# Attention on one core: queries and new keys turned by VectorE and a trip through DRAM in place of TensorE, with the second values' product, the token sums and the keys' norms moved

## The chip, the cores and the metric

The kernel is one launch on one core of a Trainium2 chip. The metric is device time in microseconds, the median of several runs. Beside it there is one profiled execution, with the times of every instruction; times of single instructions below are from it.

## What is computed

Four layers work on x, 8 blocks of 128 tokens with 512 features, and the result of each is added to x: low-rank adapters and a gated MLP, a second pair of adapters, attention with a paged cache followed by a routed low-rank layer, and a last pair. The change lies in the attention of the third layer:

```python
q = x @ Wq.T   # 32 heads of 128;  k, v: 8 heads
q, k = rope(rmsnorm(q) * qw), rope(rmsnorm(k) * kw)
kc, vc = k_cache[block_table], v_cache[block_table]      # 512 cached rows for each block
k_all, v_all = concat(kc, k), concat(vc, v)              # 640 keys, each used by 4 heads
scores = q . k_all / sqrt(128), cached rows from the block's length on set to -1e30
o = softmax(scores) . v_all
y = o @ Wo.T
```

rmsnorm divides each head's vector by the root of its mean square. All data are float32.

## The kernel before

The attention is a loop over 32 steps n in `run` (L1176). A step is one head group qd of 8 (one key head, four query heads) and one pair p of 4 (two blocks of 128 tokens, j = 0 and 1). Step n works on three steps' data at once:

- `weigh(n, j)` (L1066): scores of block j, transposed. For each of five chunks c of 128 keys, a product of the keys (features by keys, as weights) with the queries of four heads (features by 512) into a PSUM tile `st`, then Exp on ScalarE into `pT` (L1074). Chunks 0 to 3 are cached keys `kT`, chunk 4 the new keys `kn`.
- `added` (L1080): four VectorE adds over the five chunks into `part`. `divisors` (L1088): a product with ones (`sum`, L1094), reciprocal, four copies R (L1102), and three copies of R between partitions by DMA on SP's queue, then one of the sums.
- `mix(n, j)` (L1108): five products of values with `pT` into `av`, then one VectorE multiply by R into `oT` (L1116). `outputs`: VectorE sums `os` of oT.
- `project(n+1)` (L953): queries, keys and values of the next step, by a Strassen-like scheme of seven block products (`seven`, L915; tiles q_one, q_six, q_five), VectorE adds the parts (L936, L937, L968). Its token-side sums `xs` come from `tokens` (L910), four VectorE adds, in every step.
- `leave(n-1)` (L1125): the same scheme with Wo (tiles wo_one, wo_two, wo_six), added into y by VectorE (L1135) and GpSimd (L1138, L1143). Between its products `rotate(n+1)` (L986) is placed: GpSimd's and VectorE's halves of the rotation (L997, L1001) and ScalarE's squares.
- `normed(n+1)` (L1019): ScalarE's Sqrt, VectorE adds rk+vk and rq+vq (L1025), reciprocal, and a multiply of keys and of queries by it (L1029).
- `turn_cached(n+1)` (L1032): the gathered cached keys are transposed by VectorE in 32x32 blocks (L1038, tile `kt`), written to DRAM by four DMAs on SP's queue (L1042) and read back as whole transposes by one (L1045, `kT`).
- `turn(n+1)` (L1048): new keys and queries are transposed by TensorE against the identity (kTn, L1053: 2; qTp, L1060: 8), copied out of PSUM by VectorE (L1055) and ScalarE (L1062).
- `gather` (L883): eight indirect DMAs of GpSimd for values, eight for cached keys.

Tiles come from pools with a number of buffers for each tag; a new tile waits for the last user of the buffer that it takes. The order of instructions on each engine is set when the program is built: a scheduler reorders them by its own estimates, and `kept` (L847) pins an instruction to the program's order among the pinned ones of its engine.

## Time and profile before

| | us |
|---|---|
| median of 3 runs (1638.76 to 1641.55) | 1640.6 |
| the profiled execution's own time | 1622.67 |
| its span, first to last instruction | 1620.4 |
| TensorE's 8 + 2 transposes in a step: 256 of 0.280 each, 64 of 0.299; busy in all | 40.2 + 13.9 |
| ScalarE's copies qT, 64 of 0.586 | 37.5 |
| VectorE's copies kTs, 32 of 0.362 | 11.6 |
| VectorE's multiply of keys (L1029), 32 of 0.681 | 21.8 |
| VectorE's token sums xs (L907), three rows | 26.6 + 13.6 + 13.4 |
| VectorE's transposes of cached keys (L1038), 64 of 0.687 | 41.6 |
| TensorE waits for part before sum (L1094) | 19.2 in 23 waits |

The attention loop takes from about 336 us to about 1460 us of the span. A row of groups gives an instruction's line, engine, output and inputs, shape, count, busy time in all and the mean of one. An instruction's own length overlaps with its successor's on the same engine: the pitch from one start to the next is shorter (a float32 product with 512 columns is two instructions of 0.592 us at a pitch of 0.43). In the chain of waits each piece starts where its predecessor on the chain released it. DMA rows on SP show the issue alone; a transfer's end shows where somebody waits for it.

### The profile page before, as it was taken

What the parts mean: (1) busy time and instruction counts of PE and PEld (TensorE: products, weight loads), DVE (VectorE), ACT (ScalarE), POOL (GpSimd) and SP (SyncE); (2) the same over time, 40 slices, a digit from 0 to 9 for tenths busy, and PEclk for the clock granted to TensorE, in tenths of its full rate; (3) what the DMA queues carried; (4) which work ended last, traced back from release to release, by engine and by line L of the source; (5) the groups of instructions that cost most, each with busy time, mean ns of one, the idle gap of its engine ahead of it and who ended that gap; (6) DMA issues with size and microseconds to landing.
All of it is one profiled execution on the core that took longest, in us unless ns stands there. A gap on an engine that the chain in (4) does not pass through costs nothing.

```text
span 1620.4 us, 19220 instructions
## 1 busy us (share of the span) xinstructions
PE 1568.4 (97%) x6305; PEld 955.7 (59%) x6305; DVE 1074.9 (66%) x2235; ACT 564.7 (35%) x1390; POOL 818.3 (50%) x778
## 2 busy tenths in 40 slices
PE   9999998979999999999999999999999999999998
PEld 7888884445555555555555555555555555559653
DVE  4575523477878787787878777787787877743141
ACT  1111110244445544444544444544444553420210
POOL 1341107254666676666667666666765676710000
PEclk9999998999999999999999999999999999999899
DMA  9110003031323323232332223323232332311000
GB/s 299 38 41 23 1 1 103 34 116 53 111 67 102 116 69 100 68 111 75 102 106 75 94 74 104 90 88 110 71 99 71 111 100 65 122 31 64 0 20 35
DMA packets 92237, 127.98 MB, mean 79 GB/s; under 512 B 19360, under 2 KB 59488, under 8 KB 92000
## 3 DMA queue, kind: packets, MB, share of 16 engines
q1 hardware_dynamic: 73984, 89.65, 17.9%
q0 software_dynamic: 17056, 36.49, 7.5%
q8 instruction: 52, 0.85, 0.2%
q10 hardware_dynamic: 1088, 0.52, 0.1%
q14 instruction: 57, 0.47, 0.1%
HBM read 92.91 MB, written 21.10 MB: 70 GB/s over the span
## 4 chain that ended last, share of the span: by engine, by line
PE 77%; DVE 15%; POOL 3%; DMA 2%; issue 2%; ACT 1%; SPq 0%; ACTq 0%; DVEq 0%; POOLq 0%
PE st L53 10%; PE av L53 10%; PE q_six L925 8%; PE g L362 7%; PE q_one L925 5%; PE q_five L925 5%; PE wo_two L925 5%; PE dn L362 4%; DVE part L1085 4%; PE wo_one L925 3%; PE wo_six L925 3%; DVE rq L1025 3%; DVE xs L907 2%; PE z L53 2%; PE h L1574 2%
## 5 line engine op out<-in xcount | busy, mean ns | idle before, releaser
L893 POOL DMA_INDIRECT vals<-in_v_cache,kvrow_v x256 | 273.1, 1067 | 73.2 <-issue 52.1
L893 POOL DMA_INDIRECT kn<-in_k_cache,kvrow_k x256 | 267.0, 1043 | 79.9 <-issue 77.6
L53 PE MATMUL av<-pT,vals 128*128 128x512 f32 x640 | 296.2, 594 | 0.0
L53 PE MATMUL st<-qT,kT 128*128 128x512 f32 x512 | 239.1, 599 | 4.3 <-DMA kT<-turned 4.3
L53 PEld LDWEIGHTS av<-pT,vals 128*128 128x128 f32 x640 | 119.4, 191 | 137.8 <-issue 135.6
L1074 ACT ACTIVATE pT<-st,hide 128x512 f32<-128x512 f32 x256 | 169.5, 687 | 46.6 <-PE st L53 43.9
L997 POOL TENSOR_TENSOR vq<-q,txq 128x512 f32<-128x512 f32 x64 | 83.5, 1326 | 161.2 <-DVE q L968 161.2
L53 PEld LDWEIGHTS st<-qT,kT 128*128 128x128 f32 x512 | 93.6, 192 | 99.4 <-issue 80.0
L1085 DVE TENSOR_TENSOR part<-pT 128x512 f32<-128x512 f32 x128 | 85.5, 692 | 68.6 <-ACT pT L1074 68.6
L1143 POOL TENSOR_TENSOR y<-y,uo 128x512 f32<-128x512 f32 x32 | 44.1, 1379 | 115.3 <-DVE y L1135 115.3
L1062 ACT COPY qT<-qTp 128x512 f32<-128x512 f32 x64 | 37.5, 586 | 169.2 <-PE qTp L1060 169.2
L925 PE MATMUL q_one<-q,x 128*128 128x384 f32 x256 | 96.2, 498 | 0.0
L925 PE MATMUL q_six<-q_s,xs 128*128 128x384 f32 x256 | 94.3, 486 | 0.0
L1008 ACT ACTIVATE sqq<-q 128x128 f32<-128x128 f32 x256 | 79.4, 310 | 8.3 <-DVE q L968 1.5
L1116 DVE TENSOR_TENSOR oT<-av,R 128x512 f32<-128x512 f32 x64 | 44.1, 688 | 42.5 <-PE av L53 39.1
L1025 DVE TENSOR_TENSOR rq<-rq,vq 128x1024 f32<-128x1024 f32 x32 | 70.4, 2200 | 1.2 <-POOL vq L997 1.2
L925 PEld LDWEIGHTS q_six<-q_s,xs 128*128 128x128 f32 x256 | 48.6, 190 | 36.1 <-issue 4.0
L1102 DVE COPY R<-r 32x128 f32<-32x128 f32 x256 | 66.1, 258 | 3.7
L925 PE MATMUL wo_one<-o,oT 128*128 128x256 f32 x256 | 65.8, 379 | 0.0
L933 ACT COPY uq<-q_one 128x384 f32<-128x384 f32 x32 | 15.3, 479 | 144.0 <-PE q_one L925 144.0
L53 PE MATMUL st<-qT,kTs 128*128 128x512 f32 x128 | 65.5, 593 | 0.0
L925 PEld LDWEIGHTS q_one<-q,x 128*128 128x128 f32 x256 | 46.0, 189 | 31.4 <-issue 6.0
(391 smaller groups left out, 2883.5 us busy)
## 6 DMA issues: line engine op xcount, KB each, us to landing
turned<-kt SPq DMA_DIRECT2D x128, 128.0 KB
kT<-turned SPq DMA_DIRECT2D x32, 512.0 KB
R<-R SPq DMA_DIRECT2D x192, 64.0 KB
q<-in_WqT SPq DMA_DIRECT2D x8, 1024.0 KB
o<-in_WoT SPq DMA_DIRECT2D x8, 1024.0 KB
kn<-in_k_cache,kvrow_k POOLq DMA_INDIRECT x256, 2.6
vals<-in_v_cache,kvrow_v POOLq DMA_INDIRECT x256, 2.7
wd<-in_WdT SPq DMA_DIRECT2D x2, 1280.0 KB
```

The lines of the kernel that those rows point to most:

```text
L53: pe.matmul(o, lhsT, rhs, start=start, stop=stop)
L362: pe.matmul(o, lhsT, rhs, start=start, stop=stop, skip_group_check=True)
L893: kept(pool.indirect_dma_start(out=d[:, c, :], out_offset=None, in_=kc if what == "k" else vc, in_offset=bass.IndirectOffsetOnAxis(ap=kvro ...
L925: pe.matmul(o, l[:, c, :], r[:, c, :], start=start and c == 0, stop=c == 1, skip_group_check=True)
L997: kept(pool.tensor_tensor(u[:, :, :, lo : lo + 64], t[:, :, :, hi : hi + 64], wx[:, :, lo : lo + 64].unsqueeze(2).to_broadcast(part_), ALU ...
L1008: kept(act.activation(sq, t[:, j, i, :], AF.Square, accum_out=ssq[:, j, at + i : at + i + 1]))
L1025: kept(dve.tensor_tensor(r, r, u, ALU.add))
L1074: act.activation(pT[:, c, :, :].rearrange("p i t -> p (i t)"), ps, AF.Exp, bias=hide[:, b, c : c + 1] if c < 4 else 0.0,)
L1085: kept(dve.tensor_tensor(o, l, r, ALU.add))
L1102: kept(dve.tensor_copy(R[0:32, i * P : (i + 1) * P], r[32 * i : 32 * i + 32, :]))
L1116: kept(dve.tensor_tensor(S[n]["oT"][:, j].rearrange("p i t -> p (i t)"), ps, S[n]["R", j], ALU.mult))
L1143: kept(pool.tensor_tensor(t, t, u.unsqueeze(1).to_broadcast([P, 2, HW]), ALU.add))
```

## The change

1. `turn` (new form): queries and new keys lie in one tile `both` of 10 x 128; VectorE transposes it in 32x32 blocks (one instruction of 1280 elements), four DMAs write it to DRAM, one reads the queries back as `qT`, two the keys as `kTn`. The ten TensorE transposes and their three copies are gone. The block transposes use the tag `kt`, one buffer, as those of the cached keys do; `qT` and `kTn` have one buffer. `turn(n+1)` now follows `normed(n+1)`.
2. `both` takes the tag "r" that the reciprocal in `divisors` uses, one buffer.
3. Keys are not multiplied by their norm; Exp of chunk 4 takes the norm as its scale.
4. `tokens`: the sums are kept for head groups 1 to 6 (one set for each pair, computed in group 1); groups 0 and 7 compute them as before. The kept tile shares the tag of the later `yT`, whose allocation moves to its first use.
5. `mix(n, 1)` and `outputs(n)` move from step n+1 to the end of step n, and the first product of mix for j = 1 is pinned, ahead of the next scores.
6. `divisors(n, 0)` moves into `project(n+1)`, between the fourth and fifth of its seven products; `turn_cached(n+1)` moves behind `leave(n-1)`, and its VectorE transposes are always pinned.

```diff
 def tokens(n):
-        b = 2 * steps[n][1]
+        qd, p = steps[n]
+        b = 2 * p
+        if 0 < qd < NQ - 1 and p in kept_sums:
+            S[n]["A"] = kept_sums[p]
+            return
...
+        both = wk.tile([P, 2 * REP + 2, HD], F32, tag="r", name=f"r_{n}", bufs=1)
+        views = {"q": both[:, 0 : 2 * REP], "k": both[:, 2 * REP :]}
...
 def normed(n):
+        for m in "kq":
+            r, u = s["r" + m]
+            kept(dve.tensor_tensor(r, r, u, ALU.add))
+            s[m] = r
         kept(act.activation(rs, s["ssq"], AF.Sqrt, bias=eps, scale=1.0 / HD))
-        for r, u in (s["rk"], s["rq"]):
-            kept(dve.tensor_tensor(r, r, u, ALU.add))
         kept(dve.reciprocal(rs, rs))
-        for m, at, nh in (("k", REP, 1), ("q", 0, REP)):
-            r = s["r" + m][0]
-            dve.tensor_tensor(r, r, rs[:, :, at : at + nh].unsqueeze(3).to_broadcast([P, 2, nh, HD]), ALU.mult)
-            s[m] = r
+        full = [P, 2, REP, HD]
+        kept(dve.tensor_tensor(s["q"], s["q"], rs[:, :, 0:REP].unsqueeze(3).to_broadcast(full), ALU.mult))
+        s["rs"] = rs
...
+    def written(dst, t):
         for q in range(4):
-            kept(sp.dma_start(
-                turned[n, :, :, q].rearrange("b i m d -> i b m d"), t[32 * q : 32 * q + 32]
-            ))
+            kept(sp.dma_start(dst[:, :, q].rearrange("b i m d -> i b m d"), t[32 * q : 32 * q + 32]))
 def turn(n):
+        m = 2 * REP
+        t = wk.tile([P, 4, m + 2, 32], F32, tag="kt", name=f"qkt_{n}", bufs=1)
+        kept(dve.transpose(t, s["both"].rearrange("p m (b d) -> p b m d", b=4)))
+        s["qT"] = wk.tile([P, 4, m, 32], F32, tag="qT", name=f"qT_{n}", bufs=1)
+        s["kn"] = wk.tile([P, 2, 4, 32], F32, tag="kTn", name=f"kTn_{n}", bufs=1)
+        written(turned_new[n], t)
+        src = turned_new[n].rearrange("b i a m d -> (b i) a m d")
+        kept(sp.dma_start(s["qT"], src[:, :, 0:m, :]))
         for j in range(2):
-            pe.transpose(ps[:, j, :], s["k"][:, j, 0, :], ident)
...
+            kept(sp.dma_start(s["kn"][:, j], src[:, :, m + j, :]))
 def weigh(n, j):
-            mm(ps, s["kT"][:, c, 4 * j : 4 * j + 4, :] if c < 4 else s["kn"][:, j, :], s["qT"][j], True, True)
+            mm(ps, s["kT"][:, c, 4 * j : 4 * j + 4, :] if c < 4 else s["kn"][:, j],
+               s["qT"][:, :, REP * j : REP * (j + 1), :].rearrange("p a i t -> p i a t"), True, True)
...
-                bias=hide[:, b, c : c + 1] if c < 4 else 0.0,
+                **(
+                    dict(bias=hide[:, b, c : c + 1]) if c < 4
+                    else dict(bias=0.0, scale=s["rs"][:, j, REP : REP + 1])
+                ),
 def mix(n, j, pT):
+            if c == 0 and j:
+                kept(i)
 def run(pool_, end, bank):
             pT = weigh(n, 0)
             added(n, 0, pT)
-            if last:
-                mix(n - 1, 1, last)
-            divisors(n, 0)
-            if last:
-                outputs(n - 1)
             if after:
-                project(after)
+                project(after, lambda: divisors(n, 0))
+                leave(n - 1, lambda: rotate(after))
+            else:
+                divisors(n, 0)
             if n + 1 < len(steps):
                 turn_cached(n + 1)
-            if after:
-                leave(n - 1, lambda: rotate(after))
...
                 normed(after)
+                turn(after)
                 gather(after, "v")
...
             mix(n, 0, pT)
             divisors(n, 1)
-            if n + 1 < len(steps):
-                turn(n + 1)
+            mix(n, 1, last)
+            outputs(n)
```

## The prediction

> **What bounds the kernel now.** I read the page first, then the chain of waits, then one step of the attention loop engine by engine.

> ```profile
> span 1620.4 us, 19220 instructions
> ...
> PE 1568.4 (97%) x6305; PEld 955.7 (59%) x6305; DVE 1074.9 (66%) x2235; ACT 564.7 (35%) x1390; POOL 818.3 (50%) x778
> ```

> TensorE looks like the whole bound: 97% busy. The chain of waits for one step (us from the span's start, length, what) says something else:

> ```profile
> 806.09 0.03 DVE y L1135
> ...
> 806.43 0.41 DVE rk L1025
> 806.85 2.21 DVE rq L1025
> ...
> 809.22 0.70 DVE rk L1029
> 809.92 1.13 DVE rq L1029
> 811.06 0.35 DVE xs L907
> ...
> 815.30 0.42 PE sum L1094 x8
> 815.73 0.37 PE kTn L1053 x2
> 816.10 0.44 PE qTp L1060 x4
> ...
> 840.36 0.86 PE wo_six L925 x4
> ```

> For 9.21 us, from 806.09 (the last product of `leave` has ended: call it t=0) to `sum` of the second token block at 815.30, the chain runs through VectorE: adds of y, rotation, norms, token sums (811.06 to 812.5), the four `part` adds (812.52 to 815.26). TensorE has just enough other work there and idles 0.67 us. Then it is TensorE alone, 25.95 us, to the next t=0. A step is 35.16 us; one in four (the one before a change of head group) is 34.43, mean 34.98.

> Four more readings, from the timelines of VectorE, of SP's queue (twice) and of TensorE (twice): the transposes of cached keys, their way through DRAM, and what a wait does to TensorE.

> ```profile
> 800.59 1.29 DVE L1038 STREAM_TRANSPOSE kt<-kn 128x512 f32<-128x512 f32 x2
> ```
> ```profile
> 801.91 1.78 SPq L1042 DMA_DIRECT2D turned<-kt  x4
> 805.69 0.34 SPq L1045 DMA_DIRECT2D kT<-turned  x1
> ```
> ```profile
> 358.53 0.34 SPq L1045 DMA_DIRECT2D kT<-turned  x1
> ```
> ```profile
> 363.32 5.18 PE L53 MATMUL st<-qT,kT 128*128 128x512 f32 x8 [4.32 <-DMA kT<-turned]
> ```
> ```profile
> 1341.77 0.43 PE L1094 MATMUL sum<-part,ones 128*32 128x128 f32 x8 [2.56 <-DVE part L1085]
> ...
> 1343.07 1.91 PE L53 MATMUL av<-pT,vals 128*128 128x512 f32 x2
> ```

> The cached transposes lie at 800.59, before t=0, in a gap of VectorE. Four writes take 3.78 us from first issue to the read that waits for them (801.91 to 805.69). A read of 512 KB takes 4.79 us from issue (358.53 on SP's queue) to the product that waited for it (363.32), with gathers beside it. And after idling 2.56 or 4.32 us TensorE is slow for a while: two `av` instructions took 1.91 us where they otherwise take 1.02; from 1341.77 to 1345.63 2.40 us of work took 3.86, a loss of 1.46.

> [...] half speed follows idles of 2.56, 2.91, 4.3 and 4.4 us, for 3.41 us each but once, and does not follow one of 2.58 or those of 1.5 to 1.7, so phase decides. [...] the L1025 add of 1024 elements has a median of 2.29 us and lies beside GpSimd's adds into y, its minimum is 1.21.

> **The change, part by part.** The changed program was built, and its order on each engine read.

> *PE transposes go*: 2+4+4, in pitch 0.27+0.44+0.47 = 1.18 us a step, all on the chain. ScalarE's two copies and VectorE's kTs copy go too, off the chain: nothing.

> *VectorE between t=0 and sum.* Built order: y, both cached transposes (now behind the adds of y), rk+vk, rq+vq, rs, rq*rs, transpose of queries and keys, [token sums], part, sum. Removed: rk*rs 0.70 and, for the steps with kept sums, 1.45. Added: cached transposes 1.29, moved out of their gap into the chain; one transpose of 1280 elements, 1280/512 x 0.64 = 1.6 (bounds 0.8, if such a shape ran at twice the rate, and 2.0). The shared buffer kt adds a wait: this transpose may start only when the four cached writes have landed. Queued behind it on VectorE are the four part adds, and TensorE's sum waits for those. Added up: y 0.34; transposes to 1.6; rk to 2.0; rq+vq to 4.0 (2.0, because it starts 1.3 us later and meets GpSimd for less of its time; bounds 1.2 and 2.3); rs, rq*rs to 5.35; writes issued at 1.65 landed at 5.45; transpose to 7.05; part 2.74 to 9.8; sum at **9.85** where it was 9.21. With recomputed sums (seven steps, first, second and last head group) 1.45 more.

> *TensorE's order.* In most steps two score products of the second block stand ahead of `leave`, i.e. after sum. Pitch 0.86 each, so TensorE's part from sum to the next t=0 is 25.95 - 1.18 + 1.72 = 26.5. Before sum it has 8 products x 0.86 - 0.2 = 6.7 us of work: it idles 3.15 us. In the group-change step and nearly all of the seven above the two stay behind `leave`: 24.77, idle 1.45 (2.9 with recomputed sums; 9.85 + 1.45 + 24.77 = 36.1, taken as the mean below). The second `av` ahead of the next scores moves work, adds none.

> *Queries' way back.* Even steps: SP reads qT when its writes have landed: 7.1 + 4.2 (3.78 plus some for 1280-byte pieces) = 11.3, plus 4.8 = 16.1; TensorE gets there at 9.85 + 0.36 + 4.30 + 3.87 (projection products placed as filler) = 18.4. Hidden; if that filler were gone, 1.6 us of wait. Odd steps: the built order has the three R copies ahead of qT on SP, so the read waits for the sum: oT 0.65, reciprocal 0.95, R 1.1 bring VectorE to 12.6, three issues 1.78 to 14.4, the read to 19.2. TensorE arrives at 19.0 (4.5 of filler), or in the group-change step at 17.1 (2.58): waits of 0.2 and 2.1. The keys' two reads in 128-byte pieces come 0.4 and 0.9 us after and are needed 3.4 us later: hidden. No row shows such pieces; between nothing and 1.5 us a step, I take nothing. Behind qT on SP wait the keys' reads and, in even steps, R(n,1), whose user is VectorE's last oT, 2 us ahead of need.

> *Rest.* Norms of keys in Exp: bias rows 0.687 against 0.597 us, two a step, ScalarE is 35% busy: nothing (cover gone: 0.2). Strided reading of qT by TensorE: no row shows it, taken as nothing, bounds 0 and 0.1 a product. More DMA, 1.28 MB a step on queues 25% busy: in the bounds of the reads. First scores wait for a trip through DRAM, but the present 4.32 us wait at 363.32 may go: 0, bounds -6 and +6.

> *Sum.* Group-change step 24.77 + 9.85 + 2.1 = 36.7; odd 36.55; even 36.35 twice: mean 36.5 against 34.98, **+1.5 us**, for 30 steps +45. The clock: idles of 3.15 us in three steps of four[...]; I take half speed after 85% of them at 1.46 each, 1.24, and 0.4 in the fourth: 1.0 a step, +31. Together **+76**. Against the profiled execution, 1622.7 us (span 1620.4), that is 1699; the median of the runs is 1640.6, 1.1% above, so 1717.

> **Rivals.**
> - *Same waits, clock not halved*: [...] 2.58 once did nothing; against it, 2.56 did. 1640.6 + 45 = 1686.
> - *Transfers end last*: small pieces and gathers delay qT or the keys by 1 to 1.5 us in every step. Against it, the margin of 2.3 us in even steps. 1717 + 38 = 1755.
> - *Faster: VectorE's section is no longer on the chain*. TensorE has 1.18 us less. It decides at sum by t=8.2 (8.2 + 26.5 is under 34.98). For it: rq+vq at 1.2 (-0.8), the 1280 transpose at half price (-0.8) and a landing wait that vanishes (-0.1 to -0.6) give 7.7: 34.2 a step, -24 us, 1617. Against it: three low bounds at once; without the landing wait gone it stops at 8.4, no change.
> - *The change doesn't do what it says*: the built order shows the transposes gone and the trip in place.

> **Chances.** Forecast 60%; clock not halved 22%; transfers 9%; faster 6%; no change (within 0.2%, about what a measurement can tell from none) 3%. Slower then 91%. The low end is the second case with rq+vq at its minimum, 1686 - 24 = 1662; the high end the forecast with one more microsecond a step, 1747.

> **What would show it.** The waits view: PE sum <- DVE part grows from 0.67 to about 3 us a step, the largest wait of TensorE; PE's share falls to about 92%; clock slices of 9 or less through the attention part; odd steps wait for qT, even ones don't; the 1280-element row reads 1.6 us, L1025's below 2.29. I am wrong if sum starts less than 8.5 us after `leave`'s last product, or if TensorE waits longest for qT or kTn.

## The result, and the profile after

The changed kernel took 1820.5 us (median of 4 runs, 1808.3 to 1832.3), the kernel before beside it 1641.1 (1638.8 to 1642.2): ratio 1.1095, interval 1.1015 to 1.1175. The forecast was 1717, range 1662 to 1747: the right side, far too little. Of +179 us it accounts for 76.

The page of the changed kernel, span and busy time:

```profile
span 1806.8 us, 18891 instructions
...
PE 1598.5 (88%) x5985; PEld 944.1 (52%) x5985; DVE 1042.6 (58%) x2123; ACT 527.1 (29%) x1324; POOL 788.2 (44%) x778
```

TensorE's share has fallen from 97% to 88%, below the 92% that the forecast named (in a_again, below, it is 93%). Its waits (who waits for whom: us in total, times, longest):

```profile
PE sum L1115 <- DVE part L1106: 73.8, 25, 5.3
PE st L53 <- ACT pT L1092: 66.4, 23, 6.0
```

The first line is the forecast's wait, 3.0 us each time. The second was in no one's list: a score product waits for ScalarE's Exp to free a PSUM buffer. The timelines of TensorE and of ScalarE show one such place (start, length, ..., in brackets the idle time before and its releaser):

```profile
981.22 2.74 PE L53 MATMUL st<-qT,kT 128*128 128x512 f32 x6
989.57 2.07 PE L53 MATMUL st<-qT,kT 128*128 128x512 f32 x2 [5.61 <-ACT pT L1092]
```
```profile
988.83 1.84 ACT L1092 ACTIVATE pT<-st,hide 128x512 f32<-128x512 f32 x3 [7.95 <-remote]
```

Three score products have ended by 983.96, their Exp has nothing else to wait for, and yet it starts at 988.83. "remote" means that the trace shows no event that released it. So I counted the events: TensorE has 1377 instructions that raise its semaphore (from these events the profile infers who released whom), the trace holds 1221 raises; VectorE 1745 and 1482. In the profile of before the counts agree within 3. In this place TensorE's raises are late: the three scores end at 982.24, 983.10 and 983.96, and their three raises stand within 0.08 us at 988.8, the first 6.6 us behind its product. Since the ends are 0.86 us apart and the raises 0.04, this looks like signals held back and not like products that ended late; but the profile models where a product ends, so the trace doesn't prove it. VectorE's raises that are in the trace stand within 0.05 us of an instruction's end in the whole loop: of its raises some are missing, none is seen to be late.

The same kernel was therefore measured three times more, each time beside the kernel before (a_again, a_third, a_fourth below): 1704.5, 1705.1 and 1703.5 us against 1623.3, 1624.1 and 1624.3, ratios 1.0501 (1.0479 to 1.0523), 1.0504 (1.0481 to 1.0527) and 1.0488 (1.0458 to 1.0517). No raise is missing in any of their traces (a_again holds 1380 of TensorE and 1747 of VectorE), and TensorE's wait for pT is gone. They ran on three chips (numbers 1, 4 and 13); which chip the first measurement ran on is not on record. Here are a_again's first two lines of TensorE's waits:

```profile
PE sum L1115 <- DVE part L1106: 89.0, 31, 5.4
PE q_five L941 <- DVE uq L953: 8.5, 1, 8.5
```

Measured from t=0 as the forecast has it (leave's last product, VectorE's y), in the mean of 20 steps of the loop:

| us a step | before | forecast | a_again | first measurement |
|---|---|---|---|---|
| t=0 to sum | 9.03 | 9.85 | 9.90 | 9.91 |
| sum to the next t=0 | 25.95 | 27.65 (with 1.0 for the clock) | 27.80 | 31.14 |
| step | 34.98 | 37.5 | 37.70 | 41.05 |

So there are two results. The change itself costs 5.0%, +79 us from profile to profile (1701.7 against 1622.7), where +76 was forecast. And the first measurement has 3.3 us a step more, 31 x 3.3 = 104 us in all, which come with late and missing semaphore events and did not recur. Its instructions have the same lengths (Exp 687 and 686 ns, the 1280-element transpose 1511 and 1511) and the same order.

### The profile page after: what moved, and what is told of

It reads as the page before. It is cut to its first block, busy times and chain, and to the rows that moved or that the text cites. A ratio compares the mean times of both kernels' runs of the same rounds, so it can differ in the third digit from the quotient of the medians.

```text
span 1806.8 us, 18891 instructions
## 1 busy us (share of the span) xinstructions
PE 1598.5 (88%) x5985; PEld 944.1 (52%) x5985; DVE 1042.6 (58%) x2123; ACT 527.1 (29%) x1324; POOL 788.2 (44%) x778
## 4 chain that ended last, share of the span: by engine, by line
PE 61%; DVE 14%; issue 11%; another core or an unknown queue 5%; DMA 3%; ACT 2%; SPq 1%; POOL 1%; DVEq 0%; ACTq 0%; POOLq 0%
PE st L53 11%; PE av L1136 8%; PE g L362 7%; PE q_six L941 6%; PE q_five L941 4%; PE dn L362 4%; PE q_one L941 4%; PE wo_two L941 4%; DVE part L1106 2%; PE wo_one L941 2%; DVE r L1020 2%; DVE qkt L1074 2%; PE z L53 2%; DVE r L1044 2%
## 5 line engine op out<-in xcount | busy, mean ns | idle before, releaser
L53 PE MATMUL st<-qT,kT 128*128 128x512 f32 x512 | 255.0, 624 | 71.1 <-ACT pT L1092 64.5
L1136 PE MATMUL av<-pT,vals 128*128 128x512 f32 x640 | 317.2, 642 | 0.0
L896 POOL DMA_INDIRECT kn<-in_k_cache,kvrow_k x256 | 257.8, 1007 | 98.3 <-issue 75.8
L1136 PEld LDWEIGHTS av<-pT,vals 128*128 128x128 f32 x640 | 128.6, 205 | 161.9 <-issue 160.5
L53 PEld LDWEIGHTS st<-qT,kT 128*128 128x128 f32 x512 | 97.0, 197 | 181.4 <-ACT pT L1092 88.3
L1115 PE MATMUL sum<-part,ones 128*32 128x128 f32 x512 | 28.9, 299 | 87.8 <-DVE part L1106 73.8
L1115 PEld LDWEIGHTS sum<-part,ones 128*32 128x32 f32 x512 | 10.4, 111 | 133.7 <-DVE part L1106 95.3
L941 PE MATMUL q_six<-q_s,xs_all 128*128 128x384 f32 x192 | 76.9, 529 | 0.9 <-ACT pT L1092 0.9
L53 PE MATMUL st<-qT,kTn 128*128 128x512 f32 x128 | 75.9, 679 | 1.8 <-ACT pT L1092 1.8
L1121 DVE RECIPROCAL r<-sum 128x128 f32<-128x128 f32 x64 | 61.2, 956 | 18.5 <-PE sum L1115 18.0
L1123 DVE COPY R<-r 32x128 f32<-32x128 f32 x256 | 59.4, 232 | 3.9
```

The costliest lines, as they stand in the source:

```text
L53: pe.matmul(o, lhsT, rhs, start=start, stop=stop)
L896: kept(pool.indirect_dma_start(out=d[:, c, :], out_offset=None, in_=kc if what == "k" else vc, in_offset=bass.IndirectOffsetOnAxis(ap=kvro ...
L941: pe.matmul(o, l[:, c, :], r[:, c, :], start=start and c == 0, stop=c == 1, skip_group_check=True)
L1121: kept(dve.reciprocal(r, ps))
L1123: kept(dve.tensor_copy(R[0:32, i * P : (i + 1) * P], r[32 * i : 32 * i + 32, :]))
L1136: i = pe.matmul(ps, v[:, c, :], pT[:, c, :, :].rearrange("p i t -> p (i t)"), start=c == 0, stop=c == NC - 1)
```

## Experiments

All ratios are to the kernel before, measured beside each run (medians of 1623.1 to 1624.3 us). e1 to e4 were made while the 1820 us were the only measurement.

**e1_one_read.** Queries and keys in one read of whole rows; ScalarE copies the keys out.

```diff
-        kept(sp.dma_start(s["qT"], src[:, :, 0:m, :]))
-        for j in range(2):
-            kept(sp.dma_start(s["kn"][:, j], src[:, :, m + j, :]))
+        kept(sp.dma_start(s["qT"], src))
...
+            kept(act.copy(s["kn"].rearrange("p j a d -> p a j d"), s["qT"][:, :, 2 * REP :, :]))
```

> Edit to the changed kernel: queries and keys are read back from DRAM by one DMA of whole rows (5120 bytes for each partition) in place of 512 pieces of 1024 bytes and 1024 pieces of 128 bytes; ScalarE then copies the keys out into a tile of their own (about 0.4 us). Theory A (small pieces): in the trace of the changed kernel TensorE's and VectorE's semaphore events go missing or come up to 7 us late just after the 128-byte packets, and ScalarE's Exp stands idle meanwhile; without these packets the late stretches go, steps fall from a mean of 41.1 us to 36.6 to 37.9 (the undisturbed steps of the changed kernel), so 1690 to 1720 us against 1820. Rival B (order and data): Exp or the scores wait for something in the changed order, and the size of the pieces plays no part: 1800 to 1830, the waits 'st <- ACT pT' stay at about 66 us.

1709.4 us, 1.0538 (1.0521 to 1.0556): within theory A's number, and no raise missing. By itself this looked like a proof of A. It was none, as the next runs show.

**e2_idle_reads.** As e1, and the 128-byte reads are issued again into a tile nobody uses (a tile `idle` and the two removed lines with it as target).

> As the run with one read, and the two reads of keys in 128-byte pieces are issued again behind it, into a tile that nobody uses. Theory A: the 1024 packets of 128 bytes a step bring the late stretches back although nobody needs their data: 1760 to 1820 us. Rival B, or a theory in which only the arrival of the keys counts: the time of the run with one read, within 10 us (1690 to 1720 by A's number, or 1800 to 1830 if that run stayed there).

1714.0 us, 1.0552 (1.0534 to 1.0570): 5 us more by the medians, with an interval that overlaps e1's; no late stretch, no raise missing, though its fullest steps have about 4,900 DMA packets (the changed kernel's about 5,250) and as many small ones. The small packets alone are not the cause.

**e3_before_idle.** The kernel before with such reads.

```diff
+        idle = wk.tile([P, 2, 4, 28], F32, tag="kTn_idle", name=f"kTn_idle_{n}", bufs=1)
+        for j in range(2):
+            kept(sp.dma_start(idle[:, j], turned[n].rearrange("b i a m d -> (b i) a m d")[:, :, j, 0:28]))
```

> The kernel before, with two reads a step from the cached keys' DRAM tensor in 1024 pieces of 112 bytes, behind the read of kT, into a tile that nobody uses. Theory A in its strong form (such a burst by itself blocks events): 2 to 6 us in each of 31 steps, 1700 to 1820 us. Theory A in its weak form (the burst must follow the 1280-byte writes and 1024-byte reads closely): 1641 to 1660. Rival B: 1641 to 1645.

1622.4 us, 0.9992 (0.9983 to 1.0001): nothing. A burst of a thousand pieces of 112 bytes a step costs this kernel no time.

**a_again, a_third, a_fourth.** The changed kernel itself, unedited, beside other runs.

> The changed kernel itself once more, beside the others: in the first four runs the kernel before took 1623 us where it had taken 1641 beside the changed kernel, so this says what the changed kernel takes there. If the late stretches belong to the program: 1790 to 1820 us, and semaphore events go missing in every step of the trace. If they belonged to the conditions of the first measurement: about 1700 to 1720, as with one read.

> The changed kernel a third time, beside the others. It took 1820 us in the first measurement (semaphore events missing or late in every step of the attention loop) and 1704 in the second (none missing). If the first was a matter of conditions, 1700 to 1712 again, or 1800 to 1830 together with missing events; a value between without missing events would speak against that link.

> The changed kernel once more: 1700 to 1710 us without missing semaphore events, as in the two repeats; 1800 to 1830 only together with missing events, as in the first measurement.

1704.5, 1705.1, 1703.5. Theory A falls with these: the changed kernel, with all its small pieces, is as fast as e1.

**e7_q_pieces.** One read cut in two, of 1024 and of 256 bytes.

```diff
-        kept(sp.dma_start(s["qT"], src))
+        kept(sp.dma_start(s["qT"][:, :, 0:m, :], src[:, :, 0:m, :]))
+        kept(sp.dma_start(s["qT"][:, :, m:, :], src[:, :, m:, :]))
```

> The kernel with one read, with that read cut in two: the queries in 512 pieces of 1024 bytes a step as in the changed kernel, the keys in 512 pieces of 256 bytes; ScalarE copies the keys out as there. Idle reads in 128-byte pieces had cost only 5 us, so if the program's late stretches come from the queries' read in 1024-byte pieces, this takes 1770 to 1820; if they need the 128-byte pieces that TensorE waits for, or came from elsewhere, 1705 to 1720.

1708.8 us, 1.0524 (1.0503 to 1.0544): no different from e1 (1709.4), so the size of the pieces plays no part that could be measured in the 81 us (1704.5 less 1623.3) either.

**e4_tensor_turn.** The trip undone, the rest kept: `turn` is that of before, at its place after `divisors(n, 1)`, and the rotated queries and keys have a tile of their own.

> The changed kernel with TensorE's transposes of queries and keys and their copies put back at their old place, and no trip through DRAM for them; the rotated queries and keys have a tile of their own; all other parts of the change stay (second values' product ahead, kept token sums, norms in Exp, cached keys' transposes behind the adds of y). Theory A: no small pieces, no late stretches. VectorE's chain is shorter by the 1.5 us transpose and the wait for the cached keys' writes, so sum would start 8.1 to 8.5 us after leave's last product, TensorE has 1.18 us more: 34.5 to 36 us a step, 1625 to 1675 us. Rival B (the other parts of the change make the waits): 1750 to 1830.

1643.1 us, 1.0128 (1.0111 to 1.0145), within theory A's range, which says nothing of A now. What counts: without the trip 61 of the 81 us go, and the rest of the change still costs 20. From t=0 to sum it takes 8.41 us, TensorE no longer waits there in most steps, but waits 0.7 us in 28 steps for ScalarE's copy between the transposes, where before had a value product in between:

```profile
PE qTp L1081 <- ACT qT L1083: 18.9, 28, 0.7
PE sum L1119 <- DVE part L1110: 13.6, 9, 2.7
```

The orders built differ too. In e4 five score and five value products stand between leave and sum in every regular step; in a_again two of the five scores have been pulled ahead of leave in three steps of four. So the 61 us are the price of the trip together with the order that was built around it.

**p_sums, p_sums_again.** Kept token sums alone, on the kernel before.

```diff
+        if 0 < qd < NQ - 1 and p in kept_sums:
+            S[n]["A"] = kept_sums[p]
+            return
...
+            S[n]["A"] = kept_sums[p] = combine(late[1][:, p], *parts)
```

> The kernel before with one part of the change alone: token sums kept for head groups 1 to 6. Forecast's terms: VectorE's part from leave's last product to sum loses 1.45 us of 9.21, TensorE's idle 0.67 us ahead of sum goes, and steps of 35.16 fall to 34.43: 24 steps x 0.7, so 1604 to 1614 us against 1623. Rival: TensorE's work alone sets the step already and nothing is won: 1620 to 1625.

> The kernel before with kept token sums alone, beside the run above, to see which of the two is faster: 1610 to 1614 us as before.

1612.3 us, 0.9926 (0.9909 to 0.9944), and 1610.5, 0.9921 (0.9908 to 0.9934): all steps of the middle groups take 34.43 us, t=0 to sum 8.48. As worked out: VectorE's 1.45 us buy TensorE's idle 0.7, no more.

**p_mix.** The second block's value product at the end of its own step, alone, on the kernel before.

```diff
-            if last:
-                mix(n - 1, 1, last)
             divisors(n, 0)
-            if last:
-                outputs(n - 1)
...
                 turn(n + 1)
+            mix(n, 1, last)
+            outputs(n)
...
+            if c == 0 and j:
+                kept(i)
```

> The kernel before with another part alone: the second block's value product (and the output sums) at the end of its own step, its first product pinned, so ahead of the next scores. The forecast held that this moves work and adds none: 1623 within 5. Rival, from the built order: the five value products no longer lie between the next scores and the first sum, so three score products and three value products of the next step's later work are pulled forward into that place, and TensorE has 3.3 us of work ahead of the second sum in place of 8.5; VectorE's 9.2 us are laid bare: 9.2 + 31.2 = 40.4 us a step and half clock after such waits, 1780 to 1840.

1725.8 us, 1.0635 (1.0606 to 1.0664). The rival is right in kind and too large in size (1780 to 1840), because the number of products pulled ahead of leave changes from step to step: 6, 1, 3 and 1 in the built order, and I had counted a step with 6. TensorE's timeline of p_mix, from leave's last product to the second sum, in a step with 3:

```profile
849.76 0.81 PE L925 MATMUL wo_six<-o_s,oT 128*128 128x256 f32 x3
850.41 1.02 PE L53 MATMUL st<-qT,kT 128*128 128x512 f32 x2
851.27 1.02 PE L53 MATMUL st<-qT,kTs 128*128 128x512 f32 x2
852.13 4.45 PE L1115 MATMUL av<-pT,vals 128*128 128x512 f32 x10
859.83 0.43 PE L1094 MATMUL sum<-part,ones 128*32 128x128 f32 x8 [3.25 <-DVE part L1085]
```

Seven products stand ahead of sum where before has ten; the three others (scores) stand far earlier, where the value product had been. They are the same products, but VectorE's 9.2 us no longer have cover. Waits before sum are 84.3 us in place of 19.2, waits for qT's copies 11.5, and half clock takes about 18 us of TensorE's work in place of about 3.5: 65 + 11 + 14 = 90 of the 102 us. (What half clock takes is an estimate here and below: for each product that runs at half clock its pitch less the usual pitch of its kind, over the loop from its second step on.)

**e5_early_cached.** e1, the cached transposes ahead of leave again, and another buffer for the new ones.

```diff
                 project(after, lambda: divisors(n, 0))
+                turn_cached(n + 1)
                 leave(n - 1, lambda: rotate(after))
...
-        t = wk.tile([P, 4, m + 2, 32], F32, tag="kt", name=f"qkt_{n}", bufs=1)
+        t = wk.tile([P, 4, m + 2, 32], F32, tag="vq", name=f"qkt_{n}", bufs=1)
```

> The kernel with one read, with two edits: the cached keys' block transposes go back ahead of leave (into VectorE's gap), and the transpose of queries and keys has another buffer, so that it waits for no write to land. The forecast's sum: VectorE's part from leave's last product to sum falls from 9.85 by 1.29 (transposes) to 8.4, TensorE has 26.5 us from sum on, so about 35 us a step and an idle of 1.7 us that doesn't halve the clock: 1610 to 1640 us where before takes 1623. If instead the trip itself (transfers, or the queries' late return) holds the step: 1680 to 1710, hardly below the run with one read.

1705.3 us, 1.0503 (1.0481 to 1.0525): a clear miss, 4 us below e1, in the range named for a trip that holds the step, though not for that reason: no wait for the queries is among TensorE's largest. The groups of a_again and of e5, the add of 1024 elements:

```profile
L1044 DVE TENSOR_TENSOR r<-r,vq 128x1024 f32<-128x1024 f32 x32 | 54.2, 1693 | 8.9 <-POOL vq L1016 8.9
```
```profile
L1044 DVE TENSOR_TENSOR r<-r,vq 128x1024 f32<-128x1024 f32 x32 | 70.6, 2205 | 8.4 <-POOL vq L1016 8.4
```

Of 1.29 + 0.58 us taken off the path (transposes; the wait for the writes, 18.6 us in 32 transposes of a_again) the add gives back 0.51 and the multiply behind it 0.26 (1.48 for 1.22), since they start earlier and meet more of GpSimd's adds; sum comes at 8.92. And that isn't passed on: the order built for e5 pulls 3, 2, 3 and no score products ahead of leave where the changed kernel's pulls 2, 2, 2 and none, so less work is left for TensorE there, and it still waits 83.1 us before sum.

**e12_scores_behind.** The changed kernel with TensorE's order pinned.

```diff
-        into(six, a22, t4, False)
+        into(six, a22, t4, False, name.startswith("wo"))   # its products kept
...
+            if j and not c:
+                kept(i)                                    # first score product of the second block
...
-            if c == 0 and j:
+            if c == 0:
                 kept(i)                                    # first value product, both blocks
```

> The changed kernel with its order on TensorE alone altered: leave's last product, the second block's first score product and the first value product of each block are pinned in this order, so no score or value product is pulled ahead of leave. The forecast put 1.72 us of such products in three steps of four, and 1.0 of half clock, on the path: 2.7 less in some 22 steps, 1640 to 1655 us against 1705. Rival (other waits take the place, as in the pinned run with early transposes, 1680: ScalarE's table load, VectorE's adds to q_five): 1665 to 1690.

1674.2 us, 1.0312 (1.0282 to 1.0343): half of the forecast's term, and inside the rival's range. Its waits:

```profile
PE sum L1120 <- DVE part L1111: 43.0, 32, 4.5
PE st L1092 <- ACT pT L1097: 17.6, 30, 0.6
PE q_five L941 <- DVE uq L955: 16.4, 17, 8.6
```

The wait before sum halves, and half clock costs about 9 us in place of about 39. Two new waits take 0.6 and 0.5 us each time (the longest of q_five, 8.6, lies ahead of the loop and a_again has it too): all scores now come in a row and the fourth waits for an Exp behind ScalarE's table load (1.28 us in e6_pinned, which has the same pins); and VectorE's adds to q_five stand behind the part adds.

**e6_pinned** (e5 and e12's pins) and **e8_adds_first** (e6, `added(n, 0, pT)` moved into project ahead of `divisors(n, 0)`).

> As the run with early cached transposes, and the second block's first score product is pinned behind leave's last product, the first value product of each block behind the scores: two score products fill TensorE's idle time ahead of sum (0.86 us each, so 24.8 us from sum on in place of 26.5). By the forecast's terms 8.4 to 9 + 24.8, 33.3 to 34 us a step: 1570 to 1600 us, faster than before. If the queries' return then comes late (TensorE reaches the first scores 1.7 us earlier): waits for qT, 1600 to 1640.

> As the pinned run (1680 us, where TensorE waited 40 us for VectorE's adds to q_five, queued behind the part adds), with the part adds of the first block moved behind those adds in the program. If this was the wait: 1.4 to 1.8 us less in three steps of four, 1620 to 1645. If another wait takes its place (queries' read, behind the copies of R on SP's queue; ScalarE's Exp behind the table load): 1650 to 1680.

1679.6 us, 1.0336 (1.0315 to 1.0356), and 1723.1, 1.0598 (1.0573 to 1.0623): two misses, both slower than expected. In e6 TensorE waits 40.2 us for the adds to q_five (9.7 of them once, ahead of the loop, as e5 does). Moving the part adds makes it worse: it then waits at both sums (62.3 us in 61 waits) and 24.7 us for VectorE's adds to wo_two, which come later too; the adds to q_five are waited for as before (39.9).

**e11_mix_back.** The changed kernel with the value product back at its old place.

```diff
+            if last:
+                mix(n - 1, 1, last)
+                outputs(n - 1)
             if after:
                 project(after, lambda: divisors(n, 0))
...
-            mix(n, 1, last)
-            outputs(n)
```

> The changed kernel with one part undone: the second block's value product and the output sums go back behind the first scores of the next step, without a pin. That part alone cost the kernel before 102 us (p_mix). In the built order eleven products now stand ahead of the second sum (9.3 us of TensorE's work where the changed kernel has 6.7), so the wait for VectorE's 9.85 us should nearly go: 90 us of waits before sum to under 30, half clock with it. Against that, only projection products (5.2 us) cover the queries' return: by the forecast's times TensorE arrives at 15.4 and the queries at 16.1 and 19.2 in turn. Sum: 33.4 + 0.6 + about 2.2 = 36.2 a step, 1640 to 1680 us against 1705. Rival (the trip through DRAM holds the step): waits for qT of 3 us and more in every step, 1690 to 1720.

1694.7 us, 1.0442 (1.0404 to 1.0480): only 10 us won, the rival's time with waits of 1.8 us where it had 3. The first two waits say why:

```profile
PE st L53 <- DMA qT<-turned_new: 38.7, 22, 4.5
PE sum L1115 <- DVE part L1106: 32.5, 31, 3.6
```

The wait before sum falls as expected, from 89.0 to 32.5, and the queries' return takes its place. With the trip, the second value product has two jobs, ahead of sum for VectorE and behind it for the queries' way back, and can do one.

**e13_combined** and **e14_all_values.** e13 is e5 with e11's edit and the second block's copies of R on ScalarE's queue; e14 pins all five value products ahead of the second sum.

```diff
-            kept(sp.dma_start(R[32 * i : 32 * i + 32, :], R[0:32, :]))
-        kept(sp.dma_start(sums[2 * n + j : 2 * n + j + 1, :], R[0:1, :]))
+            kept((act if j else sp).dma_start(R[32 * i : 32 * i + 32, :], R[0:32, :]))
+        kept((act if j else sp).dma_start(sums[2 * n + j : 2 * n + j + 1, :], R[0:1, :]))
```

> Trip through DRAM kept, with: value product back at its old place (as in e11), cached transposes ahead of leave and a buffer of their own (as in the run with early transposes), one read of whole rows, and the second block's copies of R issued on ScalarE's queue, so that the queries' read waits for no R. VectorE's part 9.3 us, TensorE's work ahead of sum 9.3, queries at 15.6 and TensorE there at 16.5: TensorE's own work, 33.4 us, and under 1 us of waits: 1585 to 1615 us, faster than before (1624). If the waits stay (queries late, R late for the value products): 1640 to 1680.

> The combined run with one edit more: all five value products of the second block are pinned ahead of the second sum (three of five were). In the combined run TensorE waited 1.25 us a step for VectorE ahead of sum, with 1.72 us of value products behind it. If its own work now sets the step (33.5 us) and the queries come in time (15.6 us after leave's last product against 14.9): 33.6 to 34.3 us a step in place of 34.84, 1600 to 1612. If the queries' return takes the place of the wait: 1625 to 1640.

1627.3 us, 1.0021 (1.0011 to 1.0031), and 1615.1, 0.9936 (0.9920 to 0.9953). e13 misses its number by 12 us, TensorE still waiting 38.5 us before sum; e14 misses by 3. In e14 a step takes 34.5 us in the mean, and the waits are nearly gone, over the whole run:

```profile
PE q_five L941 <- DVE uq L953: 9.7, 1, 9.7
PE sum L1115 <- DVE part L1106: 9.1, 8, 2.9
PE st L53 <- DMA qT<-turned_new: 6.0, 12, 1.3
```

So the trip's costs can be covered. That the trip wins is not shown: e14 keeps the token sums as well, and these alone, beside it (p_sums_again), take 1610.5 us.

## Why the prediction was right and wrong

*The working held.* VectorE's part was put at 9.85 and took 9.90. Its pieces were less exact than their sum; the chain of waits of a_again for one step shows them:

```profile
842.99 0.88 PE wo_six L941 x4
...
844.90 0.68 DVE kt L1058
...
846.92 2.63 DMA turned_cached<-kt
...
849.68 1.51 DVE qkt L1074
851.19 1.19 DVE part L1106 x2
...
853.94 0.43 PE sum L1115 x8
854.36 6.18 PE av L1136 x10
```

t=0 is 843.9, sum comes 10.05 us later. The chain runs over the cached transposes and the landing of their writes, as written: last transpose, writes, wait, transpose of queries and keys, part adds. The transpose of 1280 elements took 1.51 us (1.6 forecast), the add L1044 1.69 (2.0), the wait for the writes was 0.58 in the mean (0.1). The last line shows the clock: ten value instructions, 4.3 us at full speed, take 6.18 after the wait of 3.22 us. Half clock costs about 39 us in a_again's loop and some 3.5 in that of before; 31 were forecast, on my estimate that half speed follows 85% of the idles. The queries' return was overrated: 2.5 us of waits in the whole run where I had 0.2 and 2.1 in two steps of four.

*Where it failed: the cost of TensorE from sum to the next t=0, "25.95 - 1.18 + 1.72 = 26.5" and 1.0 for the clock.* In the measurement on record it was 31.14, 3.3 more than in a_again. No step of the forecast has a term for it: the time between the end of a product and the raise of its semaphore was put at nothing, without a reason. What lies in that term is shown: in 22 steps of the loop TensorE has 73 us more than in a_again, 58 of them idle (the waits for pT alone 47), the rest longer work, with half speed for 82 us in place of 58; Exp starts long after the scores that release it, TensorE's raises come late, and raises are missing from the trace. What causes it is not shown. It isn't the small pieces by themselves (e2, e3, e7), and not the program alone (three repeats without). The kernel before was slower too beside that measurement, 1641 against 1623, so the conditions (the time, the chip or both) differed for both, and cost the changed kernel 6.8% where they cost the kernel before 1.1%. Missing and late events, 1221 raises of 1377 and up to 6.6 us, are all that its trace shows of the cause, and none of the three repeats had them.

*A second error, hidden in the sum.* "The second av ahead of the next scores moves work, adds none" is false: alone it costs the kernel before 102 us (p_mix). In the total of a_again it did no harm, because I had taken the score products ahead of leave from the built order, whatever put them there. Inside the change it is not the costliest part: e11 undoes it and wins 10 us, e4 keeps it and is 20 us above before. And the pulled scores aren't its consequence alone: e4 keeps it and has none ahead of leave, e11 undoes it and has four of the second block's five there. Had I asked which products fill the place that the value product leaves, I would have seen what it had covered.

*The rivals.* "Clock not halved" (1686) is refuted by a_again's 22 stretches at half speed in the loop. The prediction's "phase decides" is borne out in the loop (last section), but one of its readings is wrong: at 246.91 us in the profile of before, ahead of the loop, half speed of 6.83 us begins within an idle of 1.69, one of those that it says half speed does not follow. "Transfers end last" (1755) is refuted for the changed kernel (2.5 us of waits in a_again), and right in kind for e11 (38.7). "Faster" named t = 8.2 for sum as its point; e5 reached 8.92 and e14 9.33, and e14 is faster all the same: not because VectorE's part shrank that far, but because more of TensorE's work was put beside it.

*What stays open.* The cause of the late and missing events. And of the 81 us the parts don't add: the trip undone gives 61 back, the value product's place undone 10, TensorE's order pinned 30. They compete for the same cover, and each undoing also gave another built order.

## What to carry to other kernels

When a product is moved, ask what it covered and what will fill its place: here the same work in another order cost 6% (p_mix). Work off a busy engine is worth only what its waits give: removing 1.18 us of transposes gained nothing that was shown, even with VectorE's part covered (e14, 1615.1, against 1610.5 with the token sums alone), while 1.45 us off VectorE paid its 0.7 us of idle time at once (p_sums). And if a trace shows an engine waiting for nothing, count the events and measure again before explaining it.

## What the hardware showed

An add of 1024 elements on VectorE takes 1.69 us in the mean in a_again and 2.21 in e5, where it starts 1.3 us earlier: in most steps GpSimd's adds into y run beside it for 0.66 of its 1.74 us in a_again, for all of its 2.29 us in e5. The shortest, beside none of them, takes 1.21 (before). So work put ahead of it cost less than it takes: of e5's 1.29 + 0.58 us this add alone gave back 0.51.

A pair of DMAs with 1024 pieces of 128 bytes moved its packets in 0.9 to 2.7 us in a_again, mostly about 1.4. Such a pair, of 112 bytes, in every step cost the kernel before nothing (0.9992, e3).

The same program ran 6.8% slower once (1820.5 against 1704.5), with TensorE's semaphore events late by up to 6.6 us in the place shown.
